# A fifth query buffer for the first cross-attention unit, earlier due queries, and maxima of two self-attention units in the feed-forward

## The chip, the core and the metric

The kernel runs on one core of a Trainium2 chip. Inside the core five engines work side by side and wait for each other through semaphores: TensorE (PE, matrix products into PSUM, with weight loads shown apart as PEld), VectorE (DVE), ScalarE (ACT), GpSimd (POOL), and SyncE (SP), which here only issues DMA transfers, in the order in which they stand in the program. PSUM holds eight banks, and every matrix product goes to one of them; in this kernel a bank is free again when DVE or ACT has read it. The metric is the device time of one execution in microseconds (us).

## What is computed

Two transformer layers on x (4 samples, 512 rows, 320 features) with a context of 1601 rows of 192 features, all in float32. A layer is self-attention, cross-attention to the context, and a gated feed-forward, each behind a layer norm and with a residual sum:

```python
def _attn(x, ctx, wq, wk, wv, wo, bo, heads):
    ...
    sim = jnp.einsum('bhid,bhjd->bhij', q, k) * scale
    a = jax.nn.softmax(sim, axis=-1)
    out = jnp.einsum('bhij,bhjd->bhid', a, v)
    out = out.transpose(0, 2, 1, 3).reshape(b, n, heads * dh)
    return out @ wo + bo
...
h1 = _ln(x, n1_g, n1_b)
x = _attn(h1, h1, q1, k1, v1, o1_w, o1_b, heads) + x
h2 = _ln(x, n2_g, n2_b)
x = _attn(h2, context, q2, k2, v2, o2_w, o2_b, heads) + x
h3 = _ln(x, n3_g, n3_b)
proj = h3 @ ff_w1 + ff_b1
a, g = jnp.split(proj, 2, axis=-1)
ff = a * jax.nn.gelu(g, approximate=False) @ ff_w2 + ff_b2
return ff + x
```

There are 20 heads of 16 features. The softmax subtracts each row's maximum, so the maxima over all keys have to be known before the exponentials of a row.

## The kernel before

**Units.** The work is cut into 88 units, made in this order for each of the two layers: 20 self-attention units (4 samples by 5 groups of 4 heads), 20 cross-attention units, and 4 feed-forward units (one a sample). Counted from 0, layer 1 has self units 0 to 19, cross units 20 to 39, feed-forward 40 to 43; layer 2 has 44 to 63, 64 to 83 and 84 to 87. The word unit with a number is used so below.

**A unit's own work** (`main`). The keys come in chunks of 128: 4 chunks in a self unit, 13 in a cross unit. A chunk has two *rounds* with two heads each (lines 1270 to 1280). A round multiplies keys by queries in two passes (`st`, line 1220; the queries are split into a high and a low part) and takes off the row maxima in a third (`st<-m,units`, line 1223). ACT then takes the exponential (line 1233). After both rounds of a chunk the products with the values follow (`av`, line 1247), and POOL adds them up (line 1264).

**Maxima.** The scores are computed a second time, with queries and keys in the other places, so that DVE can take each query row's maximum over 512 keys (`sps`, line 1032, two passes; reduced at line 1051). This has to be done for a unit before that unit starts; `max_pairs` cuts it into *pairs* (two heads, 128 queries, 512 keys), 8 pairs for a self unit, 26 for a cross unit. A pair can be placed in two ways:

- *beside* a round of scores: the two heads of the scores use two of the four row strips of the TensorE array, the pair's two heads the other two. Such a round is called *paired*; a round of scores with no pair beside it is called *bare*.
- as an *extra round* of its own: two pairs, so eight `sps` products into four banks, and four reductions on DVE. In a listing it reads `sps ... x8`.

**Who decides.** Nothing is moved by a scheduler afterwards; the Python code issues everything in order. `giver` (from line 1456) plans the maxima: `ahead` holds the units whose maxima may be dealt now, `give` adds up a debt from the maxima still to be done and the rounds left until they are due, pays it with extra rounds, and puts a pair beside every round if one is at hand. A unit is at hand three rounds after the transfers of its queries and keys were issued (`at_hand`, line 1445). In feed-forward units there are no scores, so all pairs dealt there are extra rounds (`beside`, line 1321). All other steps (projections, values, output projections, norms) lie in chains with due times in rounds; `steps` takes from them what a credit allows.

**Queries.** `queries` (line 809) projects a unit's queries on TensorE (`qps`, line 815), scales them on ACT, splits them on POOL (`split`, lines 707 and 708), and two DMA transfers on SP spread them over the partitions of the unit's query buffer (line 834). There were four such buffers, taken in turn (`qbuf[i % 4]`, line 386), so a unit's queries could not be made before the unit four places earlier had been scored (`unread`, line 926). The first cross unit of each layer (units 20 and 64) is marked `early`: 13 extra or paired placements for each pair of heads have to be done within the self units ahead of it, its keys are made some eight units ahead (chain `early`), and its queries were due at the start of the unit two places ahead of it (line 938).

**Other buffers** that matter: the keys' transposed buffers `kT` and the row of maxima `m`, filled by four small transfers a unit (line 1105) that also go through SP.

Of the kernel before, what the change touches and what calls it, by code (L numbers as in the profile page):

```python
# [9 lines left out]
F32 = mybir.dt.float32  # L10
# [7 lines left out]
B, N, D = 4, 512, 320  # L18
# [5 lines left out]
P = 128  # L24
# [102 lines left out]
def kernel(ctx: ExitStack, tc: tile.TileContext, x, context, ws, out):  # L127
# [21 lines left out]
    const = ctx.enter_context(tc.tile_pool(name="const", bufs=1))  # L149
# [30 lines left out]
    for nm in nmax:  # L180
        nc.gpsimd.memset(nm[:, HG * NQ :], 0.0)
    kbuf = [const.tile([P, 4 * QT + P], F32, name=f"kT{i}") for i in range(4)]
    qbuf = [const.tile([P, 2, 2, N // 2], F32, name=f"q{i}") for i in range(4)]

    mrows = [const.tile([P, N], F32, name=f"m{i}") for i in range(2)]
    for m in mrows:
# [170 lines left out]
    units = []  # L357
# [12 lines left out]
    attn = [u for u in units if u.kind != "ff"]  # L370
    for i, u in enumerate(attn):
        u.n = i
        u.before = attn[i - 1] if i else None

        u.m = (i % (2 * B * G)) % (B * G)
        u.early = u.cross and u.m == 0


        if u.cross:
            u.kT, u.k0 = kbuf[(1, 2, 0, 3)[u.m % 4]], 0  # L380
            u.other = attn[i - (6 if u.m == 1 else 3 if u.m == 2 else 4)] if u.m else None
        else:
            part = u.m % 4 if u.m < B * G - 1 else 0
            u.kT, u.k0 = (kbuf[0], part * N) if part < 3 else (kbuf[2], 0)
            u.other = attn[i - 3] if u.m == B * G - 1 else attn[i - 4] if u.m > 3 or u.m == 3 and u.l else None
        u.qbuf = qbuf[i % 4]
        u.mrow = mrows[i % 2]


# [27 lines left out]
    def add(chain, cost, f, due, ready=yes, soon=yes):  # L417
        chains[chain].append((cost if isinstance(cost, tuple) else (cost,), due, ready, soon, f))
# [342 lines left out]
    def add_proj(u):  # L761
        wq, wk = wq2 if u.cross else wq1, wk1
        chain = "early" if u.early else "proj"

        due = lead(u) - (6 if u.cross else 10)
# [40 lines left out]
        parts = 2 if u.cross else 1  # L806
# [118 lines left out]

        def unread():

            return u.n < 4 or attn[u.n - 4].scored == attn[u.n - 4].nch

        def free():  # L930

# [2 lines left out]
        def add_queries():  # L934
            if u.g == 0 and u.cross:
                add(chain, 0.0, hold, due - 4, yes, lambda: "h" in u.own)
            for part in range(parts):
                add(chain, (0.05 + 0.427 / parts,) * 3, lambda part=part: queries(part), units[u.i - 2].start if u.early else due - 2, unread)

        if not u.cross:  # L940
            if u.i:
# [514 lines left out]
    def giver(u):  # L1456

        ahead, coming = [], []  # L1460
        for v in units[u.i + 1 : u.i + AHEAD + 1]:
            if v.kind == "ff":
                break
            coming.append(v)
            if v.i <= u.i + 2 and (v.i == u.i + 1 or u.kind != "ff") or v.early:
                ahead.append(v)
                if v.pairs is None:
                    v.pairs = max_pairs(v)
        owed = 0.0
        last = clock["round"]  # L1470

        def give(h, alone=False):
            nonlocal owed, last
            rounds = []
            went = clock["round"] - last if alone else 1
            last = clock["round"]
            total = 0
            most = 0.0
            urgent = None
            for v in coming:  # L1480
                if v not in ahead:
                    total += v.steps
                    continue
                total += left(v)


                rest = v.start - (7 if alone else 4) - clock["round"]
                if rest > 0:
                    most = max(most, (total - rest * (not alone)) / (2 * rest))
                if left(v) and (rest == 1 or alone and rest < 1):  # L1490
                    urgent = urgent or v
                    owed = max(owed, 1.0 if alone and rest > -4 else (left(v) + 1) // 2)
            owed += most * went if total else 0.0
            while owed >= 1.0 and any(left(v) for v in ahead) and not (alone and rounds and rest > -4):
                hand = [v for v in ahead if left(v) and all(v.pairs) and at_hand(v)]
                v = hand[0] if hand else next(v for v in ahead if left(v))
                if not hand and v.start - 4 - clock["round"] > 1:
                    break
                if u.kind == "self" and ahead[-1].early and urgent is None:

                    v = ahead[-1]
                    if v not in hand:
                        break
                at_once(v)
                rounds.append([f for q in v.pairs if q for f in q.popleft()])
                owed -= 1.0
            owed = min(owed, 2.0)
            for v in ahead:
                mine = v.pairs[h % 2]
                if mine and not alone and at_hand(v):  # L1510
                    return mine.popleft(), rounds
            return [], rounds

        return give
# [35 lines left out]
    for i, u in enumerate(units):  # L1550
# [9 lines left out]
        for k in (3, AHEAD):  # L1560
            v = units[i + k] if i + k < len(units) else None
# [32 lines left out]
```

## Time and profile before

| | |
|---|---|
| three runs | 2995.1, 2990.22, 2988.99 us |
| median | 2990.22 us |
| profiled execution | 2992.5 us, span 2990.7 us |
| mean granted TensorE clock | 0.994 |
| instructions | 92123 |

The span runs from the first to the last instruction; the profiled execution's own time is 1.8 us longer. The view by windows gives the busy time of every engine in a stretch of the span. The stretches used below are the units: a unit starts with its first `st` product on TensorE (or its first `fps` product in the feed-forward), found in the timeline. TensorE's busy time is a poor measure here, since a matmul that waits in the array for a bank or a strip is counted as busy; the length of a unit is the better one. In four stretches the profile shows the granted clock at half: two within the first 52 us, one of 13.65 us from 335.2 us on, and one of 3.4 us at 516.1 us.

### The profile page before, as it was taken

To read this page: it belongs to the slowest core of one execution; us is meant where nothing else is said; L and a number is where in the kernel's file an instruction comes from. 1 tells how busy PE (TensorE), PEld (TensorE's weight loads), DVE (VectorE), ACT (ScalarE), POOL (GpSimd) and SP (SyncE) were. 2 spreads that over 40 slices of the span, in tenths; PEclk is the share of its full clock that TensorE was granted. 3 is DMA by queue.
4 is the path that set the end of the run, shared out by engine and by line. 5 is a ranking of instruction groups with operands and counts; after the bars stand their busy time and mean duration, and the time that the engine had idled before them with its cause. 6 is when DMAs were issued, how large, how long until landed. Compare 5 with 4: busy or idle time off the path is not lost. (4 is left out here: it accounts for less than half of the span.)

```text
span 2990.7 us, 92123 instructions
## 1 busy us (share of the span) xinstructions
PE 2922.0 (98%) x37842; PEld 1608.0 (54%) x37842; DVE 2041.5 (68%) x4011; ACT 1954.5 (65%) x4029; POOL 1326.1 (44%) x1503
## 2 busy tenths in 40 slices
PE   8999999999999999999999999999999999999999
PEld 4455565555555555455554555555555555544555
DVE  6777778878888788422257778778878877873221
ACT  3777577788887888611148775778878878883101
POOL 3556445554555454211125564555554565541100
PEclk8999999999999999999999999999999999999999
DMA  3434221221222121300114332221221221212000
GB/s 104 130 93 114 75 67 46 65 70 36 64 70 52 48 65 28 107 11 0 32 47 102 102 90 68 65 66 31 65 66 37 54 67 39 55 40 71 12 12 14
DMA packets 221150, 178.00 MB, mean 60 GB/s; under 512 B 137652, under 2 KB 175416, under 8 KB 220728
## 3 DMA queue, kind: packets, MB, share of 16 engines
q1 hardware_dynamic: 219928, 171.05, 22.0%
q8 instruction: 297, 4.87, 0.7%
q10 hardware_dynamic: 800, 1.06, 0.1%
q14 instruction: 125, 1.02, 0.1%
HBM read 54.67 MB, written 29.56 MB: 28 GB/s over the span
## 5 line engine op out<-in xcount | busy, mean ns | idle before, releaser
L1051 DVE TENSOR_REDUCE pm<-sps 128x1 f32<-128x512 f32 x1920 | 1190.3, 681 | 108.7 <-PE sps L1032 101.9
L1032 PE MATMUL sps<-kT,q 32*128 32x512 f32 (+1 forms) x6400 | 1061.7, 403 | 17.1 <-DMA q<-stage 7.5
L1233 ACT ACTIVATE pr<-st 128x512 f32<-128x512 f32 (+1 forms) x1710 | 905.6, 603 | 193.7 <-PE st L1223 189.0
L1220 PE MATMUL st<-q,kT 32*128 32x512 f32 (+1 forms) x5440 | 927.4, 433 | 1.9 <-DVE pm L1051 1.5
L1264 POOL TENSOR_TENSOR o<-o,pr 128x512 f32<-128x512 f32 x359 | 461.0, 1284 | 635.2 <-ACT pr L1263 620.4
L1220 PEld LDWEIGHTS st<-q,kT 32*128 32x128 f32 (+1 forms) x5440 | 480.1, 180 | 350.9 <-ACT pr L1233 142.8
L1247 PE MATMUL av<-pr,vals 128*32 128x512 f32 (+1 forms) x3420 | 635.3, 608 | 27.7 <-DVE pm L1051 6.2
L1032 PEld LDWEIGHTS sps<-kT,q 32*128 32x128 f32 x6400 | 549.0, 184 | 117.2 <-DVE pm L1051 22.2
L1223 PE MATMUL st<-m,units 32*128 32x512 f32 (+1 forms) x2720 | 530.4, 391 | 1.7 <-DMA m<-turned 1.7
L1233 ACT ACTIVATE wself<-st 128x512 f32<-128x512 f32 (+1 forms) x867 | 463.3, 604 | 84.5 <-PE st L1223 81.0
L1051 DVE TENSOR_REDUCE nmax<-sps 128x1 f32<-128x512 f32 x640 | 396.6, 681 | 130.9 <-PE sps L1032 124.5
L1247 PE MATMUL av<-wself,vals 128*32 128x512 f32 (+1 forms) x1734 | 369.3, 605 | 9.0 <-DVE pm L1051 3.4
L1264 POOL TENSOR_TENSOR o<-o,wself 128x512 f32<-128x512 f32 x191 | 245.1, 1283 | 297.1 <-ACT wself L1263 296.6
L1342 PE MATMUL fps<-hT,w 128*128 128x512 f32 x640 | 283.4, 596 | 0.0
L1365 ACT ACTIVATE pr<-fps,b 128x512 f32<-128x512 f32 x80 | 54.7, 687 | 348.9 <-PE fps L1355 246.1
L1223 PEld LDWEIGHTS st<-m,units 32*128 32x128 f32 (+1 forms) x2720 | 250.0, 181 | 20.3 <-issue 1.6
L1263 ACT COPY pr<-av 128x512 f32<-128x512 f32 x359 | 220.0, 613 | 18.9 <-PE av L1247 18.5
L1342 PEld LDWEIGHTS fps<-hT,w 128*128 128x128 f32 x640 | 118.9, 190 | 148.6 <-issue 147.5
L1247 PEld LDWEIGHTS av<-pr,vals 128*32 128x32 f32 (+1 forms) x3420 | 91.1, 108 | 195.6 <-DVE pm L1051 104.9
L707 POOL TENSOR_SCALAR stage<-stage 128x256 fp32r<-128x256 f32 (+1 forms) x155 | 106.3, 686 | 146.4 <-ACT stage L857 81.6
L1164 PEld LDWEIGHTS ops<-wo,aT 112*32 112x32 f32 (+1 forms) x3072 | 98.9, 110 | 66.5 <-issue 40.6
L892 PEld LDWEIGHTS kps<-ctxT,w 32*128 32x128 f32 (+1 forms) x4992 | 112.2, 162 | 41.3 <-ACT pr L1233 17.9
(101 smaller groups left out, 3057.0 us busy)
## 6 DMA issues: line engine op xcount, KB each, us to landing
q<-stage SPq DMA_DIRECT2D x157, 256.0 KB
kT<-w SPq DMA_DIRECT2D x120, 208.0 KB
outs<-o SPq DMA_DIRECT2D x80, 256.0 KB
kT<-stage SPq DMA_DIRECT2D x78, 128.0 KB
aT<-outs SPq DMA_DIRECT2D x32, 224.0 KB
oturn<-over SPq DMA_DIRECT2D x32, 224.0 KB
kT<-w SPq DMA_DIRECT2D x40, 144.0 KB
w<-in_L_xattn_ff_w_dram SPq DMA_DIRECT2D x20, 256.0 KB
```

What stands on the lines that cost most here:

```text
L707: eng.tensor_scalar(high.bitcast(F32R), x, 1.0, None, ALU.mult)
L892: see(nc.tensor.matmul(ps[to : to + n, :PIECE], lhsT=wk_q[rows, k, u.g * GD : u.g * GD + n], rhs=first.kvT[rows, k, at : at + PIECE], star ...
L1032: see(nc.tensor.matmul(out, lhsT=u.q[rows, t // 2, e, t % 2 * P : (t % 2 + 1) * P].bitcast(F32R), rhs=u.kT[rows, keys].bitcast(F32R), star ...
L1051: see(nc.vector.tensor_reduce(to[:, j : j + 1], ps, AX.X, ALU.max, negate=(ns == 1)))
L1164: see(nc.tensor.matmul(ps[f : f + m, : D // 2], lhsT=aT[:n, k, t * P + f : t * P + f + m], rhs=wo[:n, k, cols], start=(k == 0), stop=(k == 2),
L1220: see(nc.tensor.matmul(st[:r, :], lhsT=keys, rhs=u.q[rows, :, e].bitcast(F32R), start=(e == 0), stop=False))
L1223: see(nc.tensor.matmul(st[:r, :], lhsT=units_of[rows, :r].bitcast(F32R), rhs=u.mrow[rows, :].bitcast(F32R), start=False, stop=True,))
L1233: see(nc.scalar.activation(p[:r], st[:r], AF.Exp))
L1247: see(nc.tensor.matmul(ps[j * SLOT : (j + 1) * SLOT, :], lhsT=columns_of[:r, head : head + SLOT], rhs=pr.pop((c, j))[:r, :], start=True, s ...
L1263: see(nc.scalar.copy(vo, ps))
L1264: nc.gpsimd.tensor_tensor(u.o, u.o, vo, ALU.add)
L1342: see(nc.tensor.matmul(ps, lhsT=w1[:, k, i * FF + c * P : i * FF + (c + 1) * P], rhs=u.hT[:, k, :], start=ahead and k == 0, stop=not ahead ...
```

## The change

```diff
@@ -180,7 +180,7 @@
-    qbuf = [const.tile([P, 2, 2, N // 2], F32, name=f"q{i}") for i in range(4)]
+    qbuf = [const.tile([P, 2, 2, N // 2], F32, name=f"q{i}") for i in range(5)]
@@ -383,7 +383,7 @@
-        u.qbuf = qbuf[i % 4]
+        u.qbuf = qbuf[4 if u.early else i % 4]
@@ -925,7 +925,7 @@
         def unread():
-            return u.n < 4 or attn[u.n - 4].scored == attn[u.n - 4].nch
+            return u.n < 4 or u.early or attn[u.n - 4].scored == attn[u.n - 4].nch
@@ -935,7 +935,7 @@
             for part in range(parts):
-                add(chain, (0.05 + 0.427 / parts,) * 3, lambda part=part: queries(part), units[u.i - 2].start if u.early else due - 2, unread)
+                add(chain, (0.05 + 0.427 / parts,) * 3, lambda part=part: queries(part), units[u.i - 4].start if u.early else due - 2, unread)
@@ -1462,7 +1462,7 @@
-            if v.i <= u.i + 2 and (v.i == u.i + 1 or u.kind != "ff") or v.early:
+            if v.i <= u.i + 2 and (v.i == u.i + 1 or u.kind != "ff" or units[u.i + 1].kind == "self") or v.early:
```

Units 20 and 64 write their queries to a fifth buffer, which nobody else uses, so they wait for no other unit; their queries are due four units ahead in place of two. And in unit 43, the only feed-forward unit that self units follow, the maxima of units 44 and 45 may be dealt, where it was 44 alone.

Counted in the program's order of instructions, extra rounds go from 38 to 34 and bare rounds from 25 to 17 (paired ones from 1283 to 1291). The units in which one of the counts changes, extra / bare:

| unit | 14 | 15 | 16 | 17 | 18 | 19 | 20 | 21 |
|---|---|---|---|---|---|---|---|---|
| before | 0/0 | 0/0 | 0/0 | 3/2 | 4/0 | 3/0 | 0/2 | 1/0 |
| now | 1/0 | 1/0 | 2/0 | 2/0 | 2/0 | 1/2 | 1/0 | 0/0 |

| unit | 58 | 59 | 60 | 61 | 62 | 63 | 64 | 65 |
|---|---|---|---|---|---|---|---|---|
| before | 0/0 | 0/0 | 0/0 | 2/2 | 5/0 | 3/2 | 1/2 | 1/0 |
| now | 1/0 | 1/0 | 2/0 | 2/0 | 2/0 | 1/2 | 1/0 | 0/0 |

| unit | 43 | 44 | 45 | 46 | 47 |
|---|---|---|---|---|---|
| before | 4/0 | 4/0 | 0/1 | 0/2 | 0/0 |
| now | 7/0 | 0/0 | 0/0 | 0/0 | 0/1 |

The two query steps of unit 20 stand in unit 13 now, where they stood in unit 16; those of unit 64 in unit 57, where they stood in unit 61. Some value, projection and norm steps change places with neighbours by a unit; their number stays.

TensorE in the third chunk of unit 17 before (`q_93` holds unit 17's queries, `kT_89,q_92` are keys and queries of unit 20, `kT_88,q_95` those of unit 19):

```order
L1220 MATMUL st<-q_93,kT_88 128x512 x4
L1223 MATMUL st<-m_97,units 128x512 x2
L1220 MATMUL st<-q_93,kT_88 128x512 x2
L1032 MATMUL sps<-kT_88,q_95 128x512 x2
L1220 MATMUL st<-q_93,kT_88 128x512 x2
L1032 MATMUL sps<-kT_88,q_95 128x512 x2
L1223 MATMUL st<-m_97,units 128x512 x2
L1032 MATMUL sps<-kT_89,q_92 128x512 x8
L1247 MATMUL av<-pr,vals 32x512 x4
L1032 MATMUL sps<-kT_89,q_92 128x512 x8
```

The same chunk now (`q_96` is the new buffer):

```order
L1220 MATMUL st<-q_93,kT_88 128x512 x2
L1032 MATMUL sps<-kT_89,q_96 128x512 x2
L1220 MATMUL st<-q_93,kT_88 128x512 x2
L1032 MATMUL sps<-kT_89,q_96 128x512 x2
L1223 MATMUL st<-m_98,units 128x512 x2
L1220 MATMUL st<-q_93,kT_88 128x512 x2
L1032 MATMUL sps<-kT_88,q_95 128x512 x2
L1220 MATMUL st<-q_93,kT_88 128x512 x2
L1032 MATMUL sps<-kT_88,q_95 128x512 x2
L1223 MATMUL st<-m_98,units 128x512 x2
L1032 MATMUL sps<-kT_89,q_96 128x512 x8
L1247 MATMUL av<-pr,vals 32x512 x4
```

Before, a bare round stood there, and then two extra rounds with only four value products between them. Now unit 20's pairs also lie beside scores, and one extra round stands behind a chunk.

TensorE at the end of unit 43 now (`yps`, line 1397, is the second feed-forward product, `kT_88,q_93` are keys and queries of unit 45); before, the `vps` and `yps` rows stood there without the `sps` rows:

```order
L1032 MATMUL sps<-kT_88,q_93 128x512 x8
L967 MATMUL vps<-wself,hT 32x128 x24
L1397 MATMUL yps<-w_112,hid 128x320 x5
L1397 MATMUL yps<-w_112,pr 128x320 x5
L1032 MATMUL sps<-kT_88,q_93 128x512 x8
L1397 MATMUL yps<-w_112,hid 128x320 x5
L1397 MATMUL yps<-w_112,pr 128x320 x5
L1032 MATMUL sps<-kT_88,q_93 128x512 x8
```

Three extra rounds of unit 45 lie between the last `yps` groups and right behind them; in the program before, unit 44 had four extra rounds.

SP around the moved query transfers now (`outs<-o` saves a unit's result, `m<-turned` is the row of maxima of the next unit):

```order
L1113 DMA outs_137<-o 128x512
L834 DMA q_92<-stage 128x1x512 x2
L862 DMA kT_88<-stage 128x1x256 x2
L1105 DMA m_97<-turned 8x4x32 x4
L1140 DMA oturn<-over_140 96x1x512
L834 DMA q_96<-stage 128x1x512 x2
L1113 DMA outs_137<-o 128x512
L834 DMA q_93<-stage 128x1x512 x2
L862 DMA kT_88<-stage 128x1x256 x2
L1105 DMA m_98<-turned 8x4x32 x4
```

The row `q_96` is new at this place; the others stand as they did.

## The prediction

> **What bounds the kernel now.** I read the page's busy shares first, then the costliest groups, then windows with one unit each, and last the timeline of a few stretches.
>
> ```profile
> PE 2922.0 (98%) x37842; PEld 1608.0 (54%) x37842; DVE 2041.5 (68%) x4011; ACT 1954.5 (65%) x4029; POOL 1326.1 (44%) x1503
> L1051 DVE TENSOR_REDUCE pm<-sps 128x1 f32<-128x512 f32 x1920 | 1190.3, 681 | 108.7 <-PE sps L1032 101.9
> ```
>
> PE is busy 98% of the span, but that hides waits in the array; the reductions of the maxima are the largest group of any engine. Which of the two sets the pace differs from unit to unit, so the windows decide:
>
> ```profile
> core 0: us, PE busy (x) PEld busy (x) DVE busy (x) ACT busy (x) POOL busy (x), PEclk, DMA share, GB/s
> 321.10:339.30 18.20, 17.72 (x184) 8.74 (x180) 14.96 (x28) 10.62 (x22) 5.91 (x8) 0.89 0.31 85
> 339.30:363.80 24.50, 23.73 (x391) 13.05 (x387) 19.68 (x39) 12.08 (x26) 12.81 (x13) 0.81 0.24 58
> 363.80:386.90 23.10, 22.51 (x364) 13.92 (x363) 21.41 (x48) 12.76 (x28) 6.69 (x6) 1.00 0.15 45
> 386.90:433.60 46.70, 46.08 (x803) 28.62 (x796) 34.21 (x68) 34.47 (x75) 25.22 (x24) 1.00 0.29 65
> 1529.30:1550.60 21.30, 20.66 (x234) 10.40 (x234) 21.08 (x39) 11.22 (x22) 4.66 (x6) 1.00 0.19 43
> 1656.80:1670.40 13.60, 13.32 (x188) 6.74 (x184) 10.46 (x20) 11.34 (x24) 9.49 (x9) 1.00 0.55 173
> 1756.50:1771.30 14.80, 14.62 (x216) 7.75 (x212) 10.87 (x20) 12.04 (x25) 9.07 (x9) 1.00 0.39 109
> 1787.50:1805.70 18.20, 17.73 (x312) 10.40 (x308) 12.44 (x24) 11.82 (x25) 6.46 (x6) 1.00 0.27 76
> 1805.70:1820.90 15.20, 14.18 (x219) 7.94 (x216) 10.77 (x20) 11.19 (x25) 7.23 (x10) 1.00 0.36 100
> 1820.90:1844.90 24.00, 23.50 (x397) 13.18 (x392) 23.88 (x47) 11.86 (x26) 10.86 (x11) 1.00 0.27 67
> 1844.90:1867.30 22.40, 21.65 (x386) 14.13 (x380) 19.35 (x45) 12.81 (x31) 8.91 (x9) 1.00 0.15 38
> 1867.30:1914.20 46.90, 46.27 (x776) 28.11 (x772) 36.28 (x70) 34.17 (x73) 24.05 (x23) 1.00 0.29 65
> ```
>
> These are units 17, 18, 19, 20, then 44, 52, 58, 60, then 61, 62, 63, 64. Unit 52 is a plain self unit without extra rounds: 13.6 us, DVE busy for 10.46. In unit 62, with five extra rounds, DVE is busy 23.88 of 24.0 us, in unit 44, with four, 21.08 of 21.3: there the reductions set the end, and PE waits for banks while it counts as busy. In units 58 and 60 DVE has 4 to 6 us to spare. So the extra rounds lie where they hurt, a few units behind a place where they would fit.
>
> **The price of a round.** Prices of single steps come from the timeline, from the start of a step to the start of the next:
>
> ```profile
> 327.61 0.75 PE L1220 MATMUL st<-q,kT 32*128 32x512 f32 x8
> 328.41 0.71 PE L1032 MATMUL sps<-kT,q 32*128 32x512 f32 x6
> 353.00 1.49 PE L892 MATMUL kps<-ctxT,w 32*64 32x104 f32 x96
> 354.42 0.86 PE L815 MATMUL qps<-hT,w 112*32 112x128 f32 x24
> 355.22 0.50 PE L1220 MATMUL st<-q,kT 32*128 32x512 f32 x2
> 356.75 0.67 PE L1032 MATMUL sps<-kT,q 32*128 32x512 f32 x2
> 1484.63 0.74 PE L1032 MATMUL sps<-kT,q 32*128 32x512 f32 x8
> 1485.29 3.70 PE L1342 MATMUL fps<-hT,w 128*128 128x512 f32 x8
> 1488.92 1.50 PE L849 MATMUL kps<-hT,wself 112*32 112x256 f32 x24
> 1490.36 1.98 PE L1342 MATMUL fps<-hT,w 128*128 128x512 f32 x4
> 1516.92 1.52 PE L967 MATMUL vps<-wself,hT 112*32 112x128 f32 x48
> 1518.38 0.81 PE L1397 MATMUL yps<-w,hid 128*128 128x320 f32 x2
> 1539.95 1.18 PE L967 MATMUL vps<-wself,hT 112*32 112x192 f32 x24
> 1541.07 0.50 PE L1032 MATMUL sps<-kT,q 32*128 32x512 f32 x4
> 2441.11 1.54 PE vps L985 x45
> 2790.73 1.77 PE ops L1164 x48
> 1834.46 12.01 DVE L1051 TENSOR_REDUCE pm<-sps 128x1 f32<-128x512 f32 x20
> ```
>
> The first two rows enclose two bare rounds: 0.80 us, 0.40 each; 355.22 to 356.75 are two paired ones, 0.77 each. A context key step is 1.42 us (353.00 to 354.42), the two query steps of a cross unit 0.80, a self projection 1.44, a self value step 0.73 (two in 1.46) or 1.12, a context value step 1.54, an output projection 0.89 (two in 1.77). An extra round in the feed-forward takes 0.66 us of PE (1484.63 to 1485.29), mode switches included. For DVE it is four reductions at 12.01 / 20 = 0.60, 2.40 us.
>
> Take unit 52's own steps away (two projections, one small value step) and eight paired rounds with their value products are left: 13.6 - 2.88 - 0.73 = 10.0 us. Add each dense unit's other steps, counted in the program's order, and what is left over is the price of its extra rounds:
> - unit 62: 10.0 + two context key steps 2.84 + query steps 1.60 = 14.4; left 9.6 for five.
> - unit 63: 10.0 - 0.74 (two bare rounds) + 2.84 + 0.89 + value steps 3.5 (two of 1.54, a tail estimated at 0.4) = 16.5; left 5.9 for three.
> - unit 61: 10.0 - 0.74 + 1.60 + 1.54 = 12.4; left 2.8 for two.
>
> That is 18.3 us for ten, 1.83 each: between 0.66 and 2.40, as it must be. Layer 1 in the same way: unit 17 18.2 - 10.8 = 7.4, unit 18 24.5 - 14.4 = 10.1, unit 19 23.1 - 16.3 = 6.8, together 24.3 for ten, 6.0 more than in layer 2. The clock tells why:
>
> ```profile
> 328.00:335.20 7.20, 6.82 (x60) 3.35 (x53) 6.13 (x11) 4.31 (x9) 1.27 (x1) 1.00 0.34 108
> 335.20:348.80 13.60, 12.93 (x151) 6.20 (x147) 9.85 (x17) 4.43 (x8) 2.49 (x2) 0.50 0.01 2
> ```
>
> Just behind the crowded extra rounds of unit 17, where only 60 matmuls ran in 7.2 us, the granted clock fell to half for 13.65 us; half of that, 6.8, is the most it can cost, and the 6.0 fits. The Trainium skill, TensorE: Matmul & The Clock Gate, A second HAM failure mode: psum-queue depth-cycling, says that short waits of TensorE between groups, from cycling through PSUM banks, can make the clock swing to half and back. The trace agrees in kind: few matmuls ahead of the drop, with no long idle time in PE's row.
>
> **A thinly placed extra round** has one clean price. Units 20 and 64 hold the same steps, but 64 has one extra round more and one output projection fewer: 46.9 - 46.7 + 0.89 = 1.1 us. Bounds: 0.66 (PE alone) and 1.83 (dense).
>
> **The change, part by part.**
> 1. *Extra rounds of units 20 and 64 spread out.* Of ten dense rounds in each layer, nine are left: one each in three units (14, 15, 19; 58, 59, 63), two each in three (16, 17, 18; 60, 61, 62). For singles I take 1.1. Two in a unit make 24 reductions, 14.4 us of DVE in some 17 to 19; that is nearer to the dense case, so 1.83. Sum 3 x 1.1 + 6 x 1.83 = 14.3. Layer 2 saves 18.3 - 14.3 = 4.0, layer 1 24.3 - 14.3 = 10.0, the clock's 6.0 in it.
> 2. *Unit 44's extra rounds go.* Its other work is 10.0 + 2.88 + two value steps 2.24 = 15.1, so the four cost 21.3 - 15.1 = 6.2. Three come into unit 43 at 0.66 = 2.0: DVE is free there, and the queries and keys that they read stand several groups earlier in the program. Saved 4.2.
> 3. *Borders.* Unit 20 gains one, 21 and 65 lose one each: one fewer, 1.1 saved.
> 4. *Bare rounds become paired*, eight of them, at 0.77 - 0.40 = 0.37: 3.0 lost.
> 5. *Query steps three to four units earlier*: the same two PE steps, ACT scalings, POOL splits and two transfers, so nothing net on PE. POOL is the tight one:
>
> ```profile
> 255.20:270.90 15.70, 14.74 (x179) 7.57 (x175) 14.17 (x24) 13.09 (x27) 13.65 (x15) 1.00 0.47 124
> L707 POOL TENSOR_SCALAR stage<-stage x155: 518/538/998, 39.0 to 2629.4; 128x128 fp32r<-128x128 f32 x80, 128x256 fp32r<-128x256 f32 x75
> L708 POOL TENSOR_TENSOR stage<-stage x155: 452/462/752, 40.0 to 2630.0; 128x128 f32<-128x128 f32 x80, 128x256 f32<-128x256 f32 x75
> ```
>
> In unit 13 POOL is busy 13.65 of 15.7 us, and two splits of 0.54 + 0.46 add 2.0. On SP the two transfers wait for them; behind these stand the save of a unit's result, the next queries and keys, and the row of maxima that unit 15 needs. That row has a unit's length of 15 us to arrive, and the queries' first reader stands in the third chunk of unit 14, so I take 0. Without that cover it is 2.0 a layer, 4.0 in all. A gain from POOL's relief in units 16 and 61 is as far off any path: 0.
>
> Sum: 4.0 + 10.0 + 4.2 + 1.1 - 3.0 = 16.3. Against the profiled execution's 2992.5 (span 2990.7 and 1.8 around it) that gives 2976.2, so **2976**. The profiled execution lies 2.3 over the median; I don't take that off again, since the three runs differ by 6.1, as much as one half-clock stretch, and the sum already removes the one that this profile shows.
>
> **The rivals.** Differences under 0.2%, 6 us, can hardly be told from none: faster means below 2984.2, slower above 2996.2.
> - *The spread helps, but one half-clock stretch stays* (0.13). Two extra rounds in units 16 to 18 may starve PE as unit 17 does now. For it: that drop followed three of them. Against it: none in layer 2, where five stood in one unit. 2976 + 6 = 2982.
> - *An extra round costs the same everywhere* (0.15), because the banks it holds are read by DVE in order wherever it stands. Then 18 x 1.83 = 32.9 replaces 18.3 + 24.3, with the 6.0 of the clock kept: 3.7 saved, and with parts 2 to 4 (+2.3) the time is 2992.5 - 6.0 = 2986.5, no change to speak of. The Trainium skill, TensorEngine Tiling (Array Packing), PSUM Bottleneck, says that tiling quickens TensorE but not the reading of PSUM, which may then become the limit; by that rule alone this rival holds. Against it stands the 1.1 of unit 64, and the 4 to 6 us that DVE has free in units 58 and 60.
> - *Half-clock stretches multiply* (0.10): thin waits can now occur in twelve self units in place of seven, and each that trips costs 6 us. From the fourth on, 2976 + 24 = 3000, it is slower. For it: the one drop of this kind. Against it: 24 extra rounds (units 17 to 19, 61 to 63, 44) tripped one, and the new ones are thinner.
>
> The forecast itself has 0.62; its own range is 2964 (extra rounds near 0.66: 18 x 0.66 = 11.9 in place of 28.6 would even give 2960) to 2984. With the rivals the range is 2964 to 2990. Faster 0.75, same 0.15, slower 0.10.
>
> **What would show it.** Units 62 and 18 should shrink to about 18 us and be alike, 44 to about 15, while 14, 15, 58 and 59 grow by about 1 and 16 and 60 by 2 to 4; unit 43 should grow by 2. DVE should be busy below 95% in every unit, and no half-clock stretch should stand near 335 us. I am wrong if the new rounds cost 1.8 or more each in units 14 to 16, if half-clock stretches turn up among units 13 to 19 or 57 to 63, if the `m<-turned` row comes late behind the moved transfers, or if the cross units, whose rows hardly change, change their length.

## The result, and the profile after

| | before | changed |
|---|---|---|
| median of 11 runs | 2991.41 us | 2981.66 us |
| lowest and highest | 2988.99 and 2997.13 us | 2976.8 and 2989.22 us |
| ratio, 95% interval | | 0.9969 (0.9959 to 0.9979) |
| profiled execution, its span | 2992.5, 2990.7 us | 2981.59, 2979.8 us |
| granted clock in the profiled execution | 0.994 | 0.996 |

The change makes the kernel 0.31% faster, 9.75 us between the medians. The forecast was 2976, and its range of 2964 to 2990 holds the time. Against the profiled execution the sum said 16.3 us and the profile shows 10.9. Five microseconds of the sum are missing, and the runs below show where.

The same two rows of the page after the change, busy shares and the largest group:

```profile
PE 2913.2 (98%) x37842; PEld 1601.3 (54%) x37842; DVE 2040.5 (68%) x4011; ACT 1954.2 (66%) x4029; POOL 1328.0 (45%) x1503
L1051 DVE TENSOR_REDUCE pm<-sps 128x1 f32<-128x512 f32 x1920 | 1191.0, 681 | 104.3 <-PE sps L1032 97.2
```

The counts are the same and no engine's work has changed; only where it stands. So the answer lies in the windows by unit. After the change, units 17, 18, 44, 58, 60, 62, 63, 64 and 73:

```profile
core 0: us, PE busy (x) PEld busy (x) DVE busy (x) ACT busy (x) POOL busy (x), PEclk, DMA share, GB/s
326.50:343.20 16.70, 16.45 (x224) 9.32 (x223) 14.82 (x29) 11.25 (x23) 4.46 (x5) 1.00 0.21 60
343.20:360.90 17.70, 17.40 (x381) 9.94 (x373) 15.62 (x33) 11.68 (x27) 11.50 (x11) 1.00 0.33 79
...
1522.40:1539.60 17.20, 16.11 (x208) 7.92 (x201) 13.89 (x27) 10.80 (x22) 4.47 (x5) 0.90 0.33 75
1747.10:1763.60 16.50, 16.46 (x222) 8.61 (x218) 13.33 (x25) 12.26 (x26) 9.62 (x12) 1.00 0.40 110
1780.90:1801.70 20.80, 20.36 (x328) 11.69 (x324) 17.21 (x32) 12.03 (x25) 6.78 (x7) 1.00 0.24 64
1818.40:1836.00 17.60, 17.29 (x378) 9.87 (x373) 15.53 (x33) 11.63 (x27) 11.42 (x11) 1.00 0.31 75
1836.00:1854.00 18.00, 17.99 (x324) 11.66 (x318) 14.24 (x37) 12.10 (x29) 8.95 (x9) 1.00 0.23 62
1854.00:1901.30 47.30, 46.42 (x763) 27.77 (x759) 38.32 (x75) 34.04 (x72) 23.56 (x22) 1.00 0.29 67
2253.70:2300.60 46.90, 45.85 (x628) 25.42 (x624) 38.65 (x78) 37.47 (x77) 22.40 (x31) 1.00 0.07 19
```

Unit 18 went from 24.5 to 17.7 us and unit 62 from 24.0 to 17.6, with DVE busy for 15.5 of it where it was busy for 23.9 of 24. Unit 44 went from 21.3 to 17.2. Units 58 and 60 grew by 1.7 and 2.6. The clock column reads 1.00 in units 17 and 18, which had run at 0.89 and 0.81, but 0.90 in unit 44. Unit 73, a cross unit far behind all this, is 2.6 us longer than its row of before:

```profile
2265.40:2309.70 44.30, 43.74 (x642) 25.60 (x642) 35.40 (x71) 35.68 (x76) 18.24 (x16) 1.00 0.08 20
```

The clock of unit 44 in two windows, ahead of the drop and in it:

```profile
1522.30:1525.90 3.60, 2.91 (x36) 1.32 (x32) 3.44 (x7) 1.25 (x3) 0.00 (x0) 1.00 0.36 47
1525.90:1529.30 3.40, 3.40 (x36) 1.76 (x32) 1.93 (x4) 1.30 (x3) 0.56 (x1) 0.50 0.02 0
```

A new stretch of 3.4 us at half clock lies at the start of unit 44. Besides two of 10.24 us in the first 52 us, as before, it is the only one; those at 335.2 us (units 17 and 18) and 516.1 us (unit 22) are gone.

Summed by stage, from the starts of the units (the rest, 0.5 us, was won ahead of unit 0):

| units | before, us | after, us | measured | predicted |
|---|---|---|---|---|
| 0 to 12 and 23 to 41 | | | -0.6 | 0 |
| 13 to 22 (layer 1's crowded units) | 270.0 | 262.0 | -8.0 | -9.3 |
| 42 to 56 (seam between the layers) | 361.9 | 360.5 | -1.4 | -3.5 |
| 57 to 66 (layer 2's crowded units) | 267.2 | 263.7 | -3.4 | -3.6 |
| 67 to 87 | 982.2 | 985.2 | +3.0 | 0 |

### The profile page after: what moved, and what is told of

Its sections match the earlier page's. It is cut to its first block, busy times and chain, and to the rows that moved or that the text cites. A ratio compares the mean times of both kernels' runs of the same rounds, so it can differ in the third digit from the quotient of the medians.

```text
span 2979.8 us, 92119 instructions
## 1 busy us (share of the span) xinstructions
PE 2913.2 (98%) x37842; PEld 1601.3 (54%) x37842; DVE 2040.5 (68%) x4011; ACT 1954.2 (66%) x4029; POOL 1328.0 (45%) x1503
## 4 chain that ended last, share of the span: by engine, by line
PE 80%; DVE 14%; issue 1%; ACT 1%; POOL 1%; DMA 1%; SPq 0%; ACTq 0%; POOLq 0%; DVEq 0%
PE av L1247 20%; PE st L1220 12%; PE sps L1032 10%; PE fps L1342 9%; DVE pm L1051 7%; PE yps L1397 6%; PE kps L892 4%; PE ops L1164 4%; DVE nmax L1051 3%; PE qps L815 3%; PE vps L985 3%; PE st L1223 3%; PE fps L1355 2%; PE vps L967 2%; PE kps L849 1%
## 5 line engine op out<-in xcount | busy, mean ns | idle before, releaser
L1032 PE MATMUL sps<-kT,q 32*128 32x512 f32 (+1 forms) x6400 | 1060.8, 402 | 15.2 <-DMA q<-stage 6.1
L1032 PEld LDWEIGHTS sps<-kT,q 32*128 32x128 f32 x6400 | 548.4, 184 | 113.7 <-DVE pm L1051 21.3
L1263 ACT COPY pr<-av 128x512 f32<-128x512 f32 x359 | 219.0, 610 | 16.2 <-PE av L1247 15.6
```

Source lines behind the costliest of these rows:

```text
L1032: see(nc.tensor.matmul(out, lhsT=u.q[rows, t // 2, e, t % 2 * P : (t % 2 + 1) * P].bitcast(F32R), rhs=u.kT[rows, keys].bitcast(F32R), star ...
L1263: see(nc.scalar.copy(vo, ps))
```

## The experiments

Three questions were open: whether the two halves of the change work by themselves; what an extra round costs where it stands alone and where two stand together; and what lengthened the late cross units. The runs of one kernel scatter over 10 us and more, so each experiment was read by its units as well as by its median.

**Control: the kernel before, unchanged.** No edit.

> The kernel before, unchanged, to see the mean granted clock of each of its runs beside its time. Theory (half-clock stretches are a part of the scatter and of the gain): the runs differ by some 6 us and the times fall on a line with the clock, about 25 to 30 us for each 0.01 of the mean clock, as the runs of the changed kernel do (2976.8 us at 0.998, 2989.22 at 0.993); the mean clock is lower than the changed kernel's 0.9955 by 0.001 to 0.002. Rival (the clock has no part in the gain): the same mean clock as the changed kernel's runs, and the whole difference of 9.7 us at equal clock.

Measured: 2993.32 us (12 runs, 2982.88 to 2997.02), ratio 1.0004 (0.9995 to 1.0013). Its runs lie 14 us apart, and they go with the mean granted clock: 0.998 in the run of 2982.88, 0.993 in that of 2997.02, 2.2 us for each 0.001. The changed kernel's own runs go from 2976.8 at 0.998 to 2989.22 at 0.993. Where no half-clock stretch falls, most units of the two profiles of this program agree to 0.1 us; six differ by 0.1 to 0.4 (unit 7: 20.0 and 20.5). So most of the scatter goes with the clock, and each comparison below has a part of work and a part of clock.

**The queries alone.** The fifth buffer and the earlier due time, without the new condition in the feed-forward:

```diff
-            if v.i <= u.i + 2 and (v.i == u.i + 1 or u.kind != "ff" or units[u.i + 1].kind == "self") or v.early:
+            if v.i <= u.i + 2 and (v.i == u.i + 1 or u.kind != "ff") or v.early:
```

> The fifth buffer and the earlier due queries alone, the feed-forward as before. By the prediction's terms: layer 1 10.0 and layer 2 4.0 saved, one extra round fewer at the borders 1.1, six bare rounds fewer 2.2 lost, so 12.9 saved, ratio 0.9957. By the trace of the changed kernel: units 13 to 22 save 8.0 (3.4 at half clock in unit 22 among it) and units 57 to 65 2.2, so about 8 to 10, ratio 0.997. Rival (an extra round costs the same everywhere and the clock returns): 2 to 4 saved, ratio 0.999.

Measured: 2993.3 us, ratio 1.0001 (0.9992 to 1.001). In its profiled run, 2988.89 us and one of its shorter ones, units 13 to 22 won 8.2 us, as in the full change, but units 42 to 56 lost 0.6, 57 to 66 lost 0.7 and 67 to 87 lost 3.0; over the runs nothing is left. Unit 57 shows one place where it went; it took 15.2 us before and 16.3 after the full change, and in this kernel 20.6:

```profile
1733.90:1754.50 20.60, 17.32 (x224) 8.90 (x220) 12.50 (x22) 13.89 (x29) 15.20 (x18) 0.95 0.39 104
```

Three of its waits, with total, count and longest:

```profile
ACT stage L826 <- DMA q<-stage: 3.9, 1, 3.9
PEld sps L1032 <- ACT stage L826: 3.5, 1, 3.5
PE sps L1032 <- ACT stage L826: 3.0, 1, 3.0
```

ACT waits at the scaling of the moved queries for a staging buffer that a transfer still reads; behind ACT, TensorE waits 3.0 us for a bank. Two staging buffers are taken in turn by unit 57's own queries, its keys and the moved queries, so the moved queries need the buffer of the own ones. Here are the two query steps on TensorE (`x24` the unit's own, `x48` the moved ones) and their scalings on ACT:

```profile
1741.11 1.48 PE L815 MATMUL qps<-hT,wself 112*32 112x256 f32 x24
1742.66 0.38 ACT L826 ACTIVATE stage<-qps 128x256 f32<-128x256 f32 x1 [0.68 <-PE qps L815]
1746.23 1.50 PE L815 MATMUL qps<-hT,w 112*32 112x128 f32 x48
1751.35 0.45 ACT L826 ACTIVATE stage<-qps 128x128 f32<-128x128 f32 x2 [3.93 <-DMA q<-stage]
```

From the first scaling to the second pass 8.7 us: the split, the transfer and its landing lie between. The moved step stands only 5.1 us behind the own one. In the full change:

```profile
1733.26 1.48 PE L815 MATMUL qps<-hT,wself 112*32 112x256 f32 x24
1734.81 0.39 ACT L826 ACTIVATE stage<-qps 128x256 f32<-128x256 f32 x1 [0.36 <-PE qps L815]
1743.15 1.50 PE L815 MATMUL qps<-hT,w 112*32 112x128 f32 x48
1744.54 0.47 ACT L826 ACTIVATE stage<-qps 128x128 f32<-128x128 f32 x2 [0.49 <-DMA q<-stage]
```

There the two steps stand 9.9 us apart, and the buffer is nearly free: 0.5 us of wait. POOL's timeline suggests another cause, since in the kernel with the queries alone four residual sums (line 579) stand right ahead of the split of the own queries:

```profile
1740.13 3.36 POOL L579 TENSOR_TENSOR x<-x,brow 128x320 f32<-128x320 f32 x4
1743.44 0.86 POOL L707 TENSOR_SCALAR stage<-stage 128x256 fp32r<-128x256 f32 x1
```

But this split starts 0.4 us after its scaling ends, where in the full change it takes 2.1 us, so the sums cost little here; a run below has the same stall without them. The feed-forward condition, through the plan's debts, happens to set the two query steps far enough apart. The fifth buffer is what moves the steps, not the due time: with the buffer and the due time left at two units ahead, the program has the same instructions in the same order on all five engines.

**The feed-forward condition alone.** The kernel before with one line changed:

```diff
-            if v.i <= u.i + 2 and (v.i == u.i + 1 or u.kind != "ff") or v.early:
+            if v.i <= u.i + 2 and (v.i == u.i + 1 or u.kind != "ff" or units[u.i + 1].kind == "self") or v.early:
```

> The maxima of two self units in the last feed-forward unit of layer 1 alone, the rest as before. By the prediction's terms: 6.2 saved in unit 44, 2.0 spent in unit 43, two bare rounds fewer 0.7 lost: 3.5 saved, ratio 0.9988. Units 43 to 47 go from 143.1 to about 139.6. Rival (the third extra round, behind the last second-layer product, only moves the crowding to unit 44's start and drops the clock there, as the changed kernel's trace has it at 1525.9 us): unit 44 at 17 instead of 15, 1.5 saved, ratio 0.9995.

Measured: 2994.25 us, ratio 1.001 (1.0001 to 1.0018). At the seam it does what it does in the full change: unit 43 +2.1 us, 44 -4.1 (with a half-clock stretch of 3.4 us inside), 45 -1.9, 46 +2.8. The stage from 42 to 56 won 0.8 us. Its mean granted clock over 11 runs was 0.993, below the 0.994 of the kernel before. At equal granted clock it is as long as the kernel before (2989.6 and 2989.7 us at 0.995, with 2.3 us for each 0.001). So neither half gains alone.

**One needless extra round in each of 22 self units** (1 to 11 and 45 to 55, which have hardly any). `again(u)` computes two pairs of heads' scores of unit u's own queries and keys once more, eight `sps` products and four reductions, into a scratch column that nobody reads; the next two experiments add such rounds too.

```diff
+    scratch = const.tile([P, HG], F32, name="scratch")
+    def again(u):
+        def pair(heads):
+            pss = [bank("sps") for _ in heads]
+            def one_pass(e):
+                for j, ps in zip(heads, pss):
+                    rows = slice(j * SLOT, (j + 1) * SLOT)
+                    see(nc.tensor.matmul(ps, lhsT=u.q[rows, 0, e, :P].bitcast(F32R),
+                        rhs=u.kT[rows, u.k0 : u.k0 + N].bitcast(F32R), start=(e == 0), stop=(e == 1)))
+            def reduce():
+                for j, ps in zip(heads, pss):
+                    see(nc.vector.tensor_reduce(scratch[:, j : j + 1], ps, AX.X, ALU.max))
+            return [lambda e=e: one_pass(e) for e in range(2)], reduce
+        return [lambda heads=heads: pair(heads) for heads in ((2, 3), (0, 1))]
...
             u.scored = c + 1
+            if u.kind == "self" and 1 <= u.m <= 11:
+                extra += [again(u)] * (c == 2)
```

> The kernel before with one needless extra round (eight score products, four reductions into a scratch tile, read by nobody) behind the third chunk of each of the 22 self units 1 to 11 and 45 to 55, to measure the price of a thinly placed extra round by itself. The prediction's price: 1.1 each, 24 us more. Rival (the same price everywhere): 1.83 each, 40 us more. PE alone would be 0.66 each, 14.5; DVE alone 2.4, 53.

Measured: 3038.1 us (4 runs), ratio 1.0156 (1.0142 to 1.0169). That is 46.5 us over the 2991.63 of the kernel before beside it, 2.1 a round, with some half-clock stretches in it. Units 47 and 48 before, and with one round each:

```profile
1581.80:1595.40 13.60, 13.32 (x192) 6.71 (x188) 10.44 (x20) 11.32 (x24) 6.99 (x7) 1.00 0.58 139
1595.40:1609.80 14.40, 13.13 (x191) 6.27 (x187) 11.99 (x29) 11.22 (x24) 7.99 (x12) 1.00 0.45 88
```

```profile
1607.60:1623.10 15.50, 15.21 (x196) 7.53 (x192) 12.53 (x23) 11.40 (x24) 6.97 (x7) 1.00 0.47 109
1623.10:1639.40 16.30, 15.09 (x196) 7.37 (x192) 14.14 (x31) 11.43 (x24) 6.98 (x7) 1.00 0.37 69
```

At full clock one round costs 1.9 us in each of these two. They stand at the dear end. Unit 49, before and with one round, shows what else happened:

```profile
1609.80:1624.20 14.40, 13.72 (x188) 6.69 (x184) 12.77 (x25) 11.40 (x24) 8.69 (x15) 1.00 0.33 79
```

```profile
1639.40:1659.40 20.00, 16.59 (x196) 7.80 (x192) 16.84 (x32) 11.67 (x24) 9.60 (x21) 0.91 0.27 68
```

It grew by 5.6 us, with 3.4 us at half clock in it; units 5 and 8, with such a stretch too, grew by 5.1 and 4.4. The other 19 of the 22 units ran at full clock in both profiles, and there a round costs 1.3 us on average, from 0.3 in unit 10 to 2.1 in unit 6 (unit 7, one of those that scatter, became 1.2 shorter). At equal granted clock the whole kernel pays some 42 us, 1.9 a round, with what happens in the units behind included. The room on DVE orders these prices only weakly: units 45 and 46, where DVE had 6.6 and 7.3 us to spare, pay 0.9 and 1.7, units 47 and 52, with some 3 to spare, 1.9.

**Two extra rounds in each of these units, behind the third and the fourth chunk.**

```diff
-                extra += [again(u)] * (c == 2)
+                extra += [again(u)] * (c >= 2)
```

> As with one needless extra round a unit, but two, behind the third and behind the fourth chunk of the same 22 self units (44 in all, read by nobody). One a unit took 46 us more in the median, 41 at equal clock, 1.9 each; unit by unit 1.1 to 2.1 where the clock was full. Theory (the price depends on the room that DVE has left, so it rises from the first to the second): the second costs up to DVE's 2.4, so 22 x (1.9 + 2.3) = 92 us more, ratio 1.031. Rival (the same price for each): 22 x 3.8 = 84, ratio 1.028.

Measured: 3071.96 us (4 runs), ratio 1.0271 (1.0256 to 1.0285). By the ratio that is 81 us, 1.84 for each of 44 rounds; at equal granted clock 77, 1.75 each. Units 47 and 48:

```profile
1621.60:1638.90 17.30, 16.94 (x207) 8.63 (x203) 15.02 (x28) 11.65 (x24) 6.95 (x7) 1.00 0.36 90
1638.90:1657.10 18.20, 16.53 (x207) 8.22 (x203) 16.59 (x35) 11.61 (x24) 6.95 (x7) 1.00 0.32 61
```

They take 3.7 and 3.8 us more than before. Over the same 19 units, at full clock here too, two rounds cost 2.9 us on average: 1.3 for the first, 1.6 for the second. The second is a little dearer, and far from the 2.3 of the theory.

**The same two, both behind the third chunk.**

```diff
-                extra += [again(u)] * (c >= 2)
+                extra += [again(u)] * (2 * (c == 2))
```

> The same 44 needless extra rounds, but both behind the third chunk, with one chunk's value products between them, as unit 17 has it before the change. Prediction's own step (crowding is what costs; dense 1.83 against thin 1.1): clearly dearer than two apart, by 22 x 0.7 = 16 us or more, and with more half-clock stretches. Rival (DVE's queue is the same wherever in the unit they stand): within 4 us of two apart, so that spreading them inside the same units would gain nothing, and the change's gain comes from fewer extra rounds and from other places.

Measured: 3087.63 us (4 runs), ratio 1.0317 (1.0303 to 1.0331), 15.7 us over the kernel with the two apart, 0.7 a unit. Units 47 and 48:

```profile
1631.70:1650.50 18.80, 18.32 (x204) 8.73 (x200) 15.68 (x28) 11.49 (x24) 6.97 (x7) 0.91 0.29 72
1650.50:1670.70 20.20, 18.40 (x208) 8.62 (x204) 17.60 (x38) 11.64 (x24) 7.11 (x8) 0.92 0.28 55
```

The clock column shows what crowding brings: 0.91 and 0.92, where it was 1.00 with the same rounds apart. Of the 22 units, eight have a half-clock stretch in this profile, 27.3 us in all; with the rounds apart it was two, with 6.8. Over the four runs of each the mean clock was 0.990 against 0.993. At equal clock (2.3 us for each 0.001, the slope over the runs of one kernel) about 7 of the 15.7 us are left as work, 0.3 a unit.

**The late cross units.** A theory formed on the changed profile: layer norms of cross units, which `steps` issues up to six units ahead, come nearer to the scores and lengthen unit 73. Two kernels let cross units' norms start later, four and five units ahead:

```diff
-        while norms and norms[0].i <= i + (1 if norms[0].kind == "ff" else AHEAD + 1 if norms[0].early else 6):
+        while norms and norms[0].i <= i + (1 if norms[0].kind == "ff" else AHEAD + 1 if norms[0].early else 6 if norms[0].kind == "self" else 4):
```

> The changed kernel, and the norms of the cross units are put into their chain at most four units ahead in place of six (the first cross unit of a layer keeps its nine). By the program's order the norm steps then go from units 24, 29, 68 and 73 to 27 and 28, 32, 71 and 72, and 76, and the extra rounds stay at 34. Theory (the 3.0 us that the changed kernel loses in units 66 to 83 come from the norm steps that now stand in unit 73, 46.9 us against 44.3, where the value steps and two context key steps stand too): units 67 to 87 take 982 to 983 again, the total 3 us or more below the changed kernel, ratio to the kernel before 0.995 to 0.996. Rival (the norm steps cost the same wherever they stand): as the changed kernel, 0.997.

Measured with four: 2980.73 us (6 runs, 2975.51 to 2983.6), ratio 0.996 (0.9948 to 0.9972). Units 71 and 73:

```profile
2164.00:2214.30 50.30, 47.33 (x788) 28.05 (x784) 39.49 (x82) 36.38 (x76) 25.58 (x35) 0.97 0.22 59
...
2255.70:2299.60 43.90, 43.66 (x667) 26.02 (x664) 34.43 (x66) 36.39 (x77) 17.98 (x16) 1.00 0.08 21
```

Unit 73 is back at 43.9, but unit 71 takes 50.3 where it took 45.8, 3.4 us of it at half clock (0.97). Over units 67 to 87 the sum is 984.4 against 985.2; without that stretch, at 0.4 us for each of its microseconds, it would be 983.0, which is within the theory's 982 to 983. In layer 1, though, where the norms moved as far, units 23 to 39 take 1.1 us more. So most of the time moved from one unit to another; a gain of 1 or 2 us is neither shown nor excluded.

> The same with five units ahead: the norms' statistics and scalings then lie in units 25, 30, 69 and 74 for one part and in 27, 32, 71 and 76 for the other, the transposes in 27, 32, 71 and 76. Theory: as with four, or 1 us better, since DVE's norm work is shared between two units (25 and 30 have more room than 24 and 29: 41.5 us long with DVE busy 33.7). Rival (the same wherever they stand): as the changed kernel, ratio 0.997.

Measured with five (the 4 in that line is a 5): 2980.76 us (6 runs), ratio 0.9966 (0.9954 to 0.9978). That is no different.

**The change once more,** without an edit, beside the next two:

> The changed kernel once more, to have more runs with their granted clock, and a second profile. Theory (the gain is half work, half clock): every unit as long as in the first profile within 0.1 us wherever no half-clock stretch falls; mean clock of the runs about 0.9957 (the kernel before had 0.9939 over 29 runs); median 2981 to 2983; no half-clock stretch in units 17, 18, 61 to 63. Rival (the clock of the first runs was chance): mean clock 0.994, median 2986.

Measured: 2982.21 us (5 runs), ratio 0.9966 (0.9952 to 0.9979). The gain repeats, at a mean clock of 0.997. Units 14 and 52 differ from the first profile by 0.4 and 1.1 us without a half-clock stretch, against the theory. Its profile has half-clock stretches at 155.6, 1527.7, 1985.1 and 2288.9 us besides the start, none of them in units 17, 18 or 61 to 63.

**The stall of the queries alone, undone.** In layer 2 the early queries stay out of unit 57, on top of the kernel with the queries alone:

```diff
-            return u.n < 4 or u.early or attn[u.n - 4].scored == attn[u.n - 4].nch
+            return u.n < 4 or u.early and (u.l == 0 or clock["round"] >= units[u.i - 6].start + 2) or attn[u.n - 4].scored == attn[u.n - 4].nch
```

> The queries part alone, as in the run that showed no gain, but in layer 2 the first cross unit's query steps may not stand before the second chunk of unit 58 (they stood in unit 57). By the program's order they go to unit 58, one extra round goes from 58 to 59, the extra rounds fall from 35 to 34 and the bare ones from 19 to 17, and the norm and value steps of the cross units of layer 2 stand where they stood before the change. Theory (in unit 57 the query steps met POOL's residual additions, ACT waited 3.9 us for a staging buffer and PE 3.0 for ACT): unit 57 goes from 20.6 to about 16, the total falls by 4 to 6 us against the queries part alone, ratio to the kernel before 0.998 to 0.9985. Rival (the queries part has no gain, the collision is hidden elsewhere): 1.000 again.

Measured: 2990.61 us (11 runs), ratio 0.9991 (0.9982 to 1.0). Unit 57 fell from 20.6 to 15.2 us, and unit 58 rose from 16.3 to 21.4. Unit 58 in this kernel, its waits, and its query steps:

```profile
1750.20:1771.50 21.30, 17.30 (x236) 9.15 (x232) 10.94 (x20) 12.05 (x26) 10.96 (x13) 0.84 0.30 82
ACT stage L826 <- DMA q<-stage: 4.3, 1, 4.3
...
PE sps L1032 <- ACT stage L826: 3.8, 1, 3.8
1752.57 1.48 PE L815 MATMUL qps<-hT,wself 112*32 112x256 f32 x24
1757.69 0.84 PE L815 MATMUL qps<-hT,w 112*32 112x128 f32 x24
```

It is the same wait at the same two lines, one unit later, with the two query steps again 5.1 us apart and no residual sum on POOL between the unit's start and the splits. So the stall goes with the distance of the steps, not with the sums. The clock of 0.84 is a half-clock stretch of 6.8 us that begins in the stall; unit 58 pays for both. Moving the step by a unit moved the stall and did not remove it. This run shows something else too: units 67 and 73, which take 43.1 and 46.9 us in the changed kernel and in the one with the queries alone, are back at 41.7 and 44.1, as before the change.

**The same delay in both layers, on the kernel with norms four ahead:**

```diff
-            return u.n < 4 or u.early or attn[u.n - 4].scored == attn[u.n - 4].nch
+            return u.n < 4 or u.early and clock["round"] >= units[u.i - 6].start + 2 or attn[u.n - 4].scored == attn[u.n - 4].nch
```

> The changed kernel with norms at most four units ahead, and the first cross units' query steps not before the second chunk of units 14 and 58, away from the units in which POOL is busy for 13.7 of 15.7 us. Theory: unit 13 and 57 lose 1.2 each and 14 and 58 gain as much or less, POOL's queue gets shorter: up to 2 us better than norms at four units ahead alone (ratio 0.9955). Rival: the same steps cost the same one unit later, ratio 0.996.

Measured: 2985.57 us (10 runs), ratio 0.9978 (0.9969 to 0.9988). Against the kernel with norms four ahead, units 13 and 57 became 1.3 us shorter each, but 14, 15, 58 and 59 longer by 3.4, 2.1, 2.7 and 2.1 (unit 14 with 3.4 us at half clock). In units 14 and 58 the query steps stand 5.1 us apart once more, and ACT waits 3.4 and 3.8 us for the staging buffer. By the medians, 4.8 us apart, the place that the changed kernel gives the query steps is the better one, though the intervals still meet.

No kernel beats the change for certain. The one with the norms four units ahead has the lowest median, and its interval (0.9948 to 0.9972) overlaps the change's own (0.9959 to 0.9979).

## Why the prediction was right, and where it was not

Of the sum's surplus of 5.4 us, 3.0 lie in the late cross units, 2.1 at the seam between the layers, 1.3 and 0.2 in the crowded units of the two layers; 1.1 came back elsewhere, unforecast (all rounded).

**The crowded units: right.** Units 18 and 62 shrank to 17.7 and 17.6, "about 18 us and alike"; 14, 15, 58 and 59 grew by 1.4, 1.3, 1.7 and 1.1, 16 and 60 by 2.2 and 2.6. In all of units 13 to 19 and 57 to 63 DVE is now busy 89% at most. The stage around layer 2's, 57 to 66, won 3.4 for the 3.6 predicted. Layer 1's, 13 to 22, won 8.0 for 9.3, and there the near hit has luck in it: the 8.0 contain the 3.4 us at half clock of unit 22, which the prediction didn't book.

**The price of a thinly placed round: too low.** "For singles I take 1.1" rested on one pair of units, 20 and 64, and on a corrected difference of 0.2 us between rows of 47. Put alone into 22 units, a round costs 1.3 in the units at full clock and 1.9 by the whole kernel; in the changed kernel, units 15, 58 and 59 pay 1.3, 1.7 and 1.1. For two in a unit 1.83 each was too much in places: unit 60 pays 2.6 for two. By the prediction's own way of counting, layer 2's nine rounds come to 15.3 (units 58 to 63: 1.7, 1.1, 2.6, 3.6, 3.3, 3.0) for the 14.3 taken, so part 1 was worth 3.0 there and not 4.0. An equal price of 1.83 would have made 16.5, so the measured sum lies between the forecast and that rival. The rival's total, 6.0 us of work without the clock, comes nearer to the work measured below than the forecast's 10.3, but by way of terms that it didn't have, the seam and the cross units. The argument that spare DVE time makes a round cheap is borne out only weakly by the one-round experiment. The Trainium skill, TensorEngine Tiling (Array Packing), PSUM Bottleneck, holds that tiling speeds up the products and not the reading of PSUM. The 1.3 to 1.9, above the 0.66 of the products and below the 2.40 of four reductions, agree in kind, but the reductions don't set the price alone.

**So why is the kernel faster at all?** Two things, each worth about half.
- *Work.* At equal granted clock, 0.995, the runs of before lie at about 2989.7 us and those of the change at 2985.1, an estimate from 72 and 16 runs with the slope of 2.3 us a thousandth: 4.6 us. The two profiles say nearly the same by stages, with 0.4 us taken off for each microsecond at half clock, again an estimate: units 13 to 22 won 1.2, 42 to 56 won 2.8, 57 to 66 won 3.4, the rest ahead of unit 67 won 1.1, and units 67 to 87 lost 3.0, in all 5.5. There are seven extra rounds fewer outside the feed-forward, and three more inside it, where one costs 2.1 / 3 = 0.7. The prices of rounds are too loose to make up this sum: seven at 1.3 to 1.9 are 9.1 to 13.3; less 2.1 in unit 43, 3.0 for eight bare rounds that became paired (the prediction's own price) and 3.0 in the late cross units, 1.0 to 5.2 are left.
- *Clock.* Over the same runs the mean granted clock is 0.9940 before and 0.9960 after, worth 4.6 us. The prediction booked 6.0 for the stretch at 335 us, which is gone in both profiles of the changed kernel. That the crowded rounds are the cause can be counted over all profiles. Six have the first cross units' queries in their old place, three of them with needless rounds in other units: in their units 17 to 19 and 61 to 63, twelve places, ten have half-clock stretches, 3.4 to 13.7 us each. Seven have the queries moved: of their fourteen places none has one. The two rounds together against apart point the same way. It is not a rule that settles everything: the kernel with one round a unit had a clock of 0.992 and the feed-forward half alone 0.993, though neither crowds more than before, and stretches come and go in units 7, 44, 66, 71 and 73. The Trainium skill, TensorE: Matmul & The Clock Gate, A second HAM failure mode: psum-queue depth-cycling, ties such drops to short waits between groups that cycle through PSUM banks. The ten against none agree in kind.

**Unit 44 and the seam: right in kind, short by 2.1.** Unit 43 grew by 2.1, as priced. Unit 44 lost 4.1 of the 6.2, with a new half-clock stretch of 3.4 us in it; in the kernel with the norms four ahead, where none falls there, unit 44 takes 15.6. Without that stretch (at 0.4 us for each of its microseconds, as unit 18 of before shows: 24.5 us with 9.6 at half clock, and 21.7 with 2.1 in the control) the stage would have won some 2.8 of 3.5.

**Query steps at nothing: right in this kernel, and by luck.** The stall that the prediction priced at 2.0 a layer without cover exists, at 3.0 us of TensorE in unit 57, when the feed-forward condition is left out. The prediction looked for it in SP's queue and in the row of maxima; no wait for that row showed up in units 13 to 16 or 57 to 60, and the stall sat on the staging buffer, which the unit's own queries hold until their transfer has landed. It showed in four places where the steps stand 5.1 us apart, and not in the two of the changed kernel, where they stand 10.3 us (unit 13) and 9.9 us (unit 57) apart. The prediction had no term for that distance.

**Cross units unchanged: wrong.** Units 67 to 87 took 3.0 us more, which is over half of the gap between 16.3 and 10.9. The prediction put them at nothing because their rows hardly change. Unit 73's +2.6 was cured by the norms' gate, but unit 71 grew by 4.5 in its place, so the norms are not the cause by themselves. The +2.6 and unit 67's +1.4 are there with the queries alone, and both went when in that kernel the query steps stayed out of unit 57; so these two hang on where the query steps stand. The sum of units 67 to 87 fell by no more than 1.0 with them, from 985.2 to 984.2, as other units grew. And the three kernels with needless rounds, whose queries stand in their old place, take 983.8 there where the kernel before takes 982.2. What lengthens this stage as a whole stays open.

**The two rivals with half-clock stretches** did not come true: none falls in units 17, 18 or 61 to 63 in either profile of the changed kernel, and its clock is higher, not lower. The first rival's 2982 matches the median by chance: its stretch was to stay in units 16 to 18, and the new one lies in unit 44.

## What to carry to other kernels

A price for "the same work in a less crowded place" should be measured by adding that work alone to many equal units, before a sum is built on the difference of two long rows, and all of these units have to be read: two of them gave 1.9 where 19 gave 1.3. When a change only reorders work, compare kernels at equal granted clock as well as by medians: half of this gain is clock, and a single run lies up to 7.6 us off the median. A step that is moved ahead lands behind other steps that use the same staging buffer; look at its distance from them, not only at the queue. And a likely culprit that stands next to a stall, here four residual sums on POOL, has to be looked for in the other places where the stall occurs.

## What was not expected of the hardware

The granted clock falls to half in stretches of 3.41, 6.83, 10.24 or 13.65 us, multiples of 3.41, in every profile taken here (apart from one that the end of the program cuts off). One microsecond of it costs about 0.4 us in this kernel: 2.1 us for each thousandth of the mean clock over 72 runs of the kernel before and 2.6 over 16 of the changed one (a thousandth is 3 us of the span, or 6 us at half clock), and between 0.34 (unit 66) and 0.58 (unit 7) in single units of the two profiles of the changed kernel. The prediction took half of a stretch as the most that it can cost; unit 7's 0.58 lies above that. The clock goes with most of the scatter, 84% of its variance in 72 runs of the kernel before and 87% in 16 of the changed one.

In all 13 profiles, the 3.41 us ahead of every such stretch between the first 60 us and the program's end hold the starts of 8 to 35 matmuls, where the middle value in the attention units of the kernel before is 48. That is not enough for a drop: 19% of the windows of this length there are as thin, and few are followed by one.
